# The seam between two parts of a TensorE-bound kernel: more of the second part's work woven into the first, and the seam's order written out

## The chip, the cores and the metric

The kernel runs on one NeuronCore of a Trainium2 chip. The core has TensorE (PE in the profile: matrix products, results into eight PSUM banks), VectorE (DVE), ScalarE (ACT), GpSimd (POOL) and SyncE (SP), whose queue issues nearly all DMAs here. Every engine works off its own queue in order and waits on semaphores for the others. The metric is device microseconds of the whole program, lower is better; most executions agree within 0.3%, those of this kernel within 0.05%.

## What is computed

The reference is one transformer layer over x of 16 sequences x 1024 positions x 512 channels, in float32, in two halves.

- Attention without softmax: q, k, v = x Wqkv^T + b; q and k are normalised by root mean square with gains gq, gk, rotated (rope), split into 16 heads of 32 and passed through relu. For each head, vk = sum over positions of [v, 1] k^T, and the output is vk q divided by its last row plus 1e-6. Then out = rmsnorm(attn Wout^T + b) gout, and x1 = layernorm(x + out).
- A feed-forward half with a shift in time: xk = mu_k x1 + (1 - mu_k) x1 of the position before (the same with mu_r for xr); r = sigmoid(xr W_r^T), k = relu(xk W_k^T)^2, and the result is layernorm(x1 + r * (k W_v^T)).

## The kernel before

The 16384 rows are N = 128 tiles of 128 positions; eight tiles make one sequence, of which there are NB = 16. Four tiles (512 positions) make one half-sequence s of the feed-forward, of which there are NH = 32. Every product of float32 numbers is made of three TensorE passes: each operand is split into a rounded high part (`..h`, written by ScalarE's copy) and the rest (`..l`, a VectorE or GpSimd subtraction), and high x high, high x low and low x high are added up. A 128 x 512 result over 512 channels is thus 12 matmuls of 512 columns.

**Part one** is `slot(i)` for i = 0 to 127, one slot per tile: `proj` makes q and k (24 matmuls, psq and psk), `rope` rotates them with tables that are loaded from DRAM for every slot (`tables`, one buffer for each of four), stores q to DRAM (`q_d`) and keeps k, scaled and through relu, as kh and kl. `add_kx(i - 1)` adds x^T k of the tile before to four PSUM banks (pskx, 12 matmuls). POOL keeps the sum of k over the sequence (`acc`). After a sequence's eighth tile, `finish_a` moves the four banks to SBUF (kx, high and low), `finish_s` makes the sums of k (psks, ksv), `finish_b` makes (Wv x^T) k (pskv: four groups g of four 256-wide and four 128-wide matmuls, two groups to a bank), adds the bias, and masks off what lies outside the heads, `finish_c` multiplies by Wout (psm) and stores the 512 x 512 matrix m of the sequence to DRAM (`m_d`), in four chunks. With m, the attention's output of a tile is q m. From slot 5 on, `late_weight` loads, splits and stores the feed-forward weights to DRAM, one chunk a slot.

Of **part two**, the attention's rest for a tile j is `part_q` (q through relu and divided by its denominator, VectorE), `part_qt` (four transposes, psqt, split into qth and qtl), `part_s` (a bank preset with the bias by ScalarE), `part_m` (12 matmuls, psy) and `part_y` (rmsnorm, residual, layernorm: a chain over DVE, ACT and POOL that ends with x1 in place of x). The feed-forward of half-sequence s is `part_t` (four times: `turn` makes four transposes of x1 into a bank, pst; `mix_t` makes xk or xr of one channel chunk in ScalarE and VectorE and splits it), `part_fk` (psk, relu, square), `part_fr` (psr, sigmoid) and `part_fv` (psv, gate, residual, layernorm, store). In the loop over s, attention runs two half-sequences ahead, one tile per step u, and `ffn` says which parts stand in which step.

Part two starts inside part one: at FIRST = 46 and every STEP = 8 slots, tile j = 0 to 6 (NPRE = 7) has its q and x loaded and `part_q`; for j below NDONE = 4 also `part_qt`, and one slot later `part_s`, `part_m`, `part_y`. Between the parts (the transition, lines 765 to 915) come the last add_kx and finish_*, the rest of tiles 4 to 9, and the first half-sequence's turns, mixes and psk.

Order: a scheduler places the instructions on each engine by a model of their times; `in_order(engine)` ties the instructions traced inside it to the order of the text. `issue_after(load.ins)` keeps DMAs behind a given one on SP. Memory comes from pools, taken and given back by the text; `ring` gives tile n of a tag one of `outer` buffers of an early pool or one of `inner` buffers of a pool opened later. `bank(name)` hands out the eight PSUM banks in turn: four from the pool `psum`, and once pskx is done four from `psumb`.

The lines that the change and the prediction touch: constants (22 to 26), `bank` (120), `load_m`, `load_ks`, `load_x` (190 to 206), `add_kx` (471 to 479), `finish_b` (532 to 543), the woven part of `slot` (739 to 755), `turn` and `mix_t` (778 to 803), `part_fk` (815), the transition (833 to 861), `ffn_first` (897) and the loop (903 to 934).

## Time and profile before

| | |
|---|---|
| median of three runs | 2735.54 us (2735.19 to 2736.36) |
| the profiled execution | 2735.11 us, span 2733.3 us |
| matmuls | 12558 |
| PE, PEld, DVE, ACT, POOL busy | 99%, 82%, 80%, 69%, 26% of the span |
| mean granted TensorE clock | 0.996 |
| moved by DMA | 431.18 MB, mean 158 GB/s |

The span runs from the first to the last instruction; the time of the execution is 1.8 us more. All times below are microseconds from the span's start. Part one takes the first 1195 us. A matmul's end in the profile is modelled: 512-wide ones last some 0.39 us each and start 0.227 apart, so a busy PE is not yet one at its peak, and a gap between two ends a little short of the time lost. PE's idle time before an instruction is put down to the engine that ended the wait. The row "granted clock" says what share of full speed TensorE's throttle allowed in a stretch. A line like L553 is a line of the kernel before; in the changed kernel the lines are shifted.

### The profile page before, as it was taken

The numbers are of one execution on the slowest core, as the hardware profiler recorded it, in microseconds if no ns is written. First come the engines' busy times: TensorE is split into PE (matmuls) and PEld (weight loads), VectorE is DVE, ScalarE is ACT, GpSimd is POOL, SyncE is SP. The second block draws the span as 40 slices with busy tenths as digits, with TensorE's granted clock in tenths as the row PEclk, the third lists the DMA queues.
The fourth block names the chain that finished last, engine by engine and source line by source line (L and its number), as shares of the span: only waits on it lengthen the run. The fifth ranks groups of instructions, "written<-read, shape, count | busy, mean of one in ns | idle before, by whom it ended". The sixth has DMA issues, their size and how long they took to land.

```text
span 2733.3 us, 40180 instructions
## 1 busy us (share of the span) xinstructions
PE 2693.3 (99%) x12558; PEld 2232.9 (82%) x12558; DVE 2190.7 (80%) x4879; ACT 1885.8 (69%) x3822; POOL 701.0 (26%) x801
## 2 busy tenths in 40 slices
PE   8999999999999999989999999999999999999998
PEld 6787888888888888867888888888888888888887
DVE  7887887888888877777887888888887888888874
ACT  6666665566666666567777777777777777777775
POOL 5222222222222222224322222222222222222221
PEclk9999999999999999999999999999999999999999
DMA  7698777777777777764222231323223232313210
GB/s 237 220 301 292 245 232 254 229 236 225 222 242 242 237 231 238 230 211 156 95 85 91 92 112 60 115 85 106 72 93 112 67 104 89 120 56 106 78 53 37
DMA packets 230862, 431.18 MB, mean 158 GB/s; under 512 B 24548, under 2 KB 24804, under 8 KB 230648
## 3 DMA queue, kind: packets, MB, share of 16 engines
q1 hardware_dynamic: 230352, 428.08, 48.7%
q8 instruction: 99, 1.62, 0.2%
q14 instruction: 115, 0.94, 0.1%
q10 hardware_dynamic: 296, 0.53, 0.1%
HBM read 313.15 MB, written 115.38 MB: 157 GB/s over the span
## 4 chain that ended last, share of the span: by engine, by line
PE 85%; DVE 6%; DMA 4%; issue 2%; ACT 2%; POOL 0%; SPq 0%; DVEq 0%; POOLq 0%; ACTq 0%
PE psk L178 13%; PE psv L178 13%; PE psr L178 13%; PE psy L178 12%; PE psq L407 9%; PE pskx L473 9%; PE psk L407 9%; PE pst L163 2%; PE psqt L163 2%; PE psm L553 1%; PE pskv L516 1%; DVE t L437 1%; DVE ro L439 1%; DMA m_d<-m 1%; DMA tab<-tab_d 1%
## 5 line engine op out<-in xcount | busy, mean ns | idle before, releaser
L178 PE MATMUL psk<-mkh,w_k 128*128 128x512 f32 x1024 | 333.3, 397 | 0.0
L178 PE MATMUL psv<-w_v,kah 128*128 128x512 f32 x1024 | 321.8, 395 | 0.0
L178 PE MATMUL psy<-mb,qth 128*128 128x512 f32 x1024 | 319.9, 389 | 0.2 <-ACT qth L233 0.2
L178 PE MATMUL psr<-w_r,mrh 128*128 128x512 f32 x1024 | 318.6, 396 | 0.0
L458 POOL TENSOR_TENSOR acc<-acc,ro 128x512 f32<-128x512 f32 x96 | 157.2, 1637 | 289.9 <-ACT ro L450 214.9
L178 PEld LDWEIGHTS psy<-mb,qth 128*128 128x128 f32 x1024 | 192.0, 188 | 40.2 <-ACT qth L233 0.4
L178 PEld LDWEIGHTS psk<-mkh,w_k 128*128 128x128 f32 x1024 | 192.2, 189 | 39.2
L142 POOL TENSOR_TENSOR rstd_all<-ss,mhalf 128x2 f32<-128x2 f32 x128 | 93.3, 729 | 501.2 <-DVE ss L444 481.0
L178 PEld LDWEIGHTS psr<-w_r,mrh 128*128 128x128 f32 x1024 | 188.8, 188 | 36.8
L178 PEld LDWEIGHTS psv<-w_v,kah 128*128 128x128 f32 x1024 | 187.8, 188 | 36.4
L800 POOL TENSOR_TENSOR mkl<-mixk,mkh 128x512 fp32r<-128x512 f32 x128 | 166.6, 1302 | 182.8 <-ACT mkh L799 182.8
L407 PE MATMUL psq<-wqk_h,xh 128*128 128x512 f32 x512 | 202.3, 395 | 6.4 <-ACT psq L157 4.6
L407 PE MATMUL psk<-wqk_h,xh 128*128 128x512 f32 x512 | 199.7, 390 | 1.8 <-ACT psk L157 1.7
L407 PE MATMUL psq<-wqk_l,xh 128*128 128x512 f32 x512 | 200.6, 392 | 0.7 <-DVE wqk_l L607 0.7
L178 PE MATMUL psk<-mkl,w_k 128*128 128x512 f32 x512 | 200.6, 392 | 0.0
L178 PE MATMUL psv<-w_v,kal 128*128 128x512 f32 x512 | 200.1, 391 | 0.0
L407 PE MATMUL psq<-wqk_h,xl 128*128 128x512 f32 x512 | 199.9, 390 | 0.0
L178 PE MATMUL psy<-mb,qtl 128*128 128x512 f32 x512 | 199.5, 390 | 0.1
L407 PE MATMUL psk<-wqk_h,xl 128*128 128x512 f32 x512 | 199.5, 390 | 0.0
L407 PE MATMUL psk<-wqk_l,xh 128*128 128x512 f32 x512 | 199.3, 389 | 0.0
L178 PE MATMUL psr<-w_r,mrl 128*128 128x512 f32 x512 | 196.7, 393 | 0.0
L142 POOL TENSOR_TENSOR yrs<-yss,mhalf 128x1 f32<-128x1 f32 x128 | 70.7, 552 | 383.5 <-DVE yss L273 275.3
(182 smaller groups left out, 7165.7 us busy)
## 6 DMA issues: line engine op xcount, KB each, us to landing
tab<-tab_d SPq DMA_DIRECT2D x480, 256.0 KB, 4.2
xt<-in_xt_dram SPq DMA_DIRECT2D x128, 256.0 KB, 4.0
xn<-in_x_dram SPq DMA_DIRECT2D x128, 256.0 KB, 3.7
q_d<-ro SPq DMA_DIRECT2D x128, 256.0 KB, 3.9
m_d<-m SPq DMA_DIRECT2D x64, 512.0 KB, 5.9
mb<-m_d SPq DMA_DIRECT2D x64, 512.0 KB, 7.0
q<-q_d SPq DMA_DIRECT2D x128, 256.0 KB, 2.9
x<-in_x_dram SPq DMA_DIRECT2D x128, 256.0 KB, 2.8
```

The costliest lines, as they stand in the source:

```text
L142: G.tensor_tensor(dst, src, mhalf[:, 0 : src.shape[1]], ALU.pow)
L163: T.matmul(ps[:, n * P : (n + 1) * P], lhsT=b, rhs=ident, is_transpose=True, start=(n == 0), stop=(n == NC_ - 1), skip_group_check=True,)
L178: T.matmul(ps, lhsT=a[u][:, rows], rhs=b[w][:, cols], start=(afresh and c == 0 and k == 0), stop=(c == n - 1 and k == 2), skip_group_check ...
L407: T.matmul(ps, lhsT=a[i][:, c, :], rhs=w_qk[b][:, c, cols], start=(not seeds and c == 0 and n == 0), stop=(seeds and c == NC_ - 1 and n == 2),
L437: V.tensor_mul(t2, ps[j], tab.pop((i, j, 1)))
L439: V.tensor_add(halves(r), halves(ps[j]), halves(t2)[:, :, ::-1, :])
L458: G.tensor_add(acc[b], acc[b], k)
L473: T.matmul(ps_kx[b][c], lhsT=a[:, c * P : (c + 1) * P], rhs=r, start=(t == 0 and n == 0), stop=(t == 7 and n == 2),)
L516: T.matmul(ps, lhsT=w_a["h"][:, c, cols], rhs=kx[:, c, g, :, :].rearrange("p two n -> p (two n)"), start=(g % 2 == 0 and c == 0), stop=Fal ...
L553: T.matmul(ps, lhsT=a[:, g, :], rhs=w_o[r][:, g, :], start=(n == 0), stop=(n == 2))
L800: (V if n == "r" and s != 1 else G).tensor_sub(ml, m, f32(mh))
```

## The change

More of part two goes into part one. FIRST is 30 instead of 46, and all eight tiles of the first sequence (NPRE = 8) are brought to x1 in part one. x1 of tiles 4 to 7 is stored to DRAM there (`x1_d`) and loaded again at the end of the transition. Three tiles of the second sequence (NQ = 3: tiles 8, 9, 10) have their q and x loaded and `part_q`, tile 8 also `part_qt`. A sequence's m is loaded one chunk a slot (slots 26 to 29 and 90 to 93) instead of four chunks at once. x has buffers in three places now: four and three in the early pool, four in the late one; weights are staged through the three (`xw`).

In the transition only tile 8's `part_m` and `part_y` are left of attention. Its order is fixed on TensorE (from the last slot on) and on ScalarE, VectorE and GpSimd: three turns and their mixes for k stand around the last `add_kx`; then `part_m(8)`, the finish steps, the fourth turn and mix, `part_y(8)`, psk00, the mixes for r, and psk01 to psk03 with `finish_c` between. `mix_t` is cut in two halves (`mix_a`, `mix_b`), `bank` takes a wished bank, and the pools of several tiles are exchanged so that w_k and w_r have other places; w_r is loaded after the finish steps. In `ffn_first` the products for r move forward by a step.

`add_kx` does a sequence's last tile bank by bank, three passes each, instead of pass by pass over the four banks. `finish_b` reads a PSUM bank only when both its groups are done.

The core of the diff:

```diff
-NPRE = 7
-FIRST, STEP = 46, 8
-NDONE = 4
-XA = 7
-XB = 4
+NPRE = 8
+NQ = 3
+FIRST, STEP = 30, 8
...
     def load_m(b, c):
-        ms[b, c] = ring("m", NC_ * b + c, NC_, 2, [P, 2, DIM], F32R, f"mb{b}{c}")
+        n = NC_ * b + c + (2 if b > 0 else 0)
+        ms[b, c] = ring("m", n, NC_, 2, [P, 2, DIM], F32R, f"mb{b}{c}")
...
-    def load_x(j):
-        xs[j] = ring("x", j, XA, XB, [P, DIM], F32, f"x{j}")
-        nc.sync.dma_start(out=xs[j], in_=x[j])
+    def load_x(j, src=None, early=False):
+        if early and j >= NT:
+            xs[j] = tp.tile([P, DIM], F32, tag="xw", bufs=3, name=f"xw{j}")
+        else:
+            xs[j] = x_tile(j)
+        nc.sync.dma_start(out=xs[j], in_=x[j] if src is None else src)
...
-            for n, (a, r) in enumerate(((h, kh), (l, kh), (h, kl))):
-                for c in range(NC_):
-                    T.matmul(
...
+            order = [(p, c) for p in three for c in range(NC_)]
+            if t == 7:
+
+                order = [(three[n], c) for c in range(NC_) for n in (0, 1, 2)]
+            for (n, a, r), c in order:
...
-                if g % 2 == 0:
-                    kv = te.tile([P, 2, P], F32, tag="kv", bufs=1, name=f"kv{b}{g}")
-                V.scalar_tensor_tensor(
-                    kv[:, g % 2, :], ks[:, cols], bv[:, g : g + 1], ps[:, 0:P], ALU.mult, ALU.add
-                )
                 if g % 2 == 1:
...
+                    for n in (g - 1, g):
+                        V.scalar_tensor_tensor(
+                            kv[:, n % 2, :],
...
+            if j + 1 in (0, NPRE) and late_by >= STEP - NC_:
+
+                with tc.issue_after(load.ins):
+                    load_m((j + 1) // 8, late_by - (STEP - NC_))
...
-                if late_by == 2 and j < NDONE:
+                if late_by == 2 and j < NPRE:
                     part_s(j)
                     part_y(j, part_m(j))
-
+                    if j >= NT:
+                        x1_d[j] = dram.tile([P, DIM], F32, name=f"x1_d{j}")
+                        nc.sync.dma_start(out=x1_d[j], in_=xs.pop(j))
...
+        end.enter_context(in_order(mybir.EngineType.PE))
+        slot(N - 1)
...
+            by_v = c == 3 if s == 0 and n == "k" else n == "r" and s != 1
+            (V if by_v else G).tensor_sub(ml, m, f32(mh))
...
         load_w("k", cb)
-        load_w("r", cb)
-        load_ks(1)
-        y5 = rest(NDONE)
+        chain = ctx.enter_context(ExitStack())
+        for e in ("Activation", "DVE", "Pool"):
+            chain.enter_context(in_order(getattr(mybir.EngineType, e)))
+        for c in range(3):
+            turn(0, c, c)
+        y8 = bank(f"psy{NPRE}", 3)
+        S.copy(y8, b_out)
+        seeds[NPRE] = y8
+        mix_a(0, 0, "k")
+        mix_a(0, 1, "k")
+        mix_b(0, 0, "k")
+        mix_a(0, 2, "k")
+        mix_b(0, 1, "k")
         add_kx(N - 1)
-        part_y(NDONE, y5)
+        part_m(NPRE)
         tk_ctx.close()
         finish_a(NB - 1)
+        mix_b(0, 2, "k")
         pa_ctx.close()
...
-        part_y(NDONE + 1, rest(NDONE + 1))
+        banks[0] = 4
         finish_s(NB - 1)
         finish_b(NB - 1)
-        first = 2 * NT
+        turn(0, 3)
+        mix_t(0, 3, "k")
         tx_ctx.close()
         wb = ctx.enter_context(tc.tile_pool(name="workb", reuse_waits="tile", bufs=1))
+        own["ks"] = wb
+        load_w("r", wb)
+        part_y(NPRE, y8)
+        part_fk(0, 0, 4)
         for c in range(NC_):
-            part_t(0, c)
-        part_y(NDONE + 2, rest(NDONE + 2))
-        for j in range(NPRE, first + 2):
-            load_q(j)
-        for g in range(NC_):
-            finish_c(NB - 1, g)
+            mix_t(0, c, "r")
+        chain.close()
+        part_fk(0, 1)
+        finish_c(NB - 1, 0)
+        finish_c(NB - 1, 1)
+        part_fk(0, 2)
+        finish_c(NB - 1, 2)
+        finish_c(NB - 1, 3)
+        part_fk(0, 3)
+        end.close()
...
+    for j in range(NT, NPRE):
+        load_x(j, src=x1_d[j])
+    load_w("v", wc)
```

More of the change, by code (lines that the diff above doesn't have):

```diff
@@ L118, with bank @@
     banks = [0]
-    def bank(name):
+    def bank(name, k=None):
+        if k is not None:
+            banks[0] = k
         k = banks[0] % 8
@@ L190, in load_m @@
     def load_m(b, c):
-        ms[b, c] = ring("m", NC_ * b + c, NC_, 2, [P, 2, DIM], F32R, f"mb{b}{c}")
+        n = NC_ * b + c + (2 if b > 0 else 0)
+        ms[b, c] = ring("m", n, NC_, 2, [P, 2, DIM], F32R, f"mb{b}{c}")
         nc.sync.dma_start(out=f32(ms[b, c]), in_=m_d[b][:, :, c, :])
     def load_ks(b):
-        ksb[b] = ring("ks", b, 1, 1, [P, DIM], F32, f"ksb{b}")
+        ksb[b] = ring("ks", b + (b > 0), 1, 1, [P, DIM], F32, f"ksb{b}")
         nc.sync.dma_start(
@@ L202, in load_q, with x_tile @@
         nc.sync.dma_start(out=qs[j], in_=q_d[j])
-    def load_x(j):
-        xs[j] = ring("x", j, XA, XB, [P, DIM], F32, f"x{j}")
-        nc.sync.dma_start(out=xs[j], in_=x[j])
+    def x_tile(j):
+        k = j % 11
+        if k < NT:
+            return tp.tile([P, DIM], F32, tag="x", bufs=NT, name=f"x{j}")
+        if k < 2 * NT:
+            return own["x"].tile([P, DIM], F32, tag="x", bufs=NT, name=f"x{j}")
+        return tp.tile([P, DIM], F32, tag="xw", bufs=3, name=f"x{j}")
+    def load_x(j, src=None, early=False):
[4 more added lines that the diff above has]
+        nc.sync.dma_start(out=xs[j], in_=x[j] if src is None else src)
     def heads(tl):
@@ L278, in part_y @@
         layernorm(xs[j], sm, f"a{j}")
-    def rest(j):
-        part_s(j)
-        part_qt(j)
-        return part_m(j)
     with ExitStack() as a_ctx:
@@ L329, with split_w @@
         w_o = {h: te.tile([P, NC_, DIM], F32R, name=f"wout_{h}") for h in "hl"}
-        def split_w(hi, lo, src, low, dma, tag="x", bufs=XA):
+        def split_w(hi, lo, src, low, dma, tag="xw", bufs=3):
             w = tp.tile([P, DIM], F32, tag=tag, bufs=bufs, name="wstage")
@@ L470, in add_kx @@
                 ]
-            for n, (a, r) in enumerate(((h, kh), (l, kh), (h, kl))):
-                for c in range(NC_):
-                    T.matmul(
-                        ps_kx[b][c],
-                        lhsT=a[:, c * P : (c + 1) * P],
-                        rhs=r,
-                        start=(t == 0 and n == 0),
-                        stop=(t == 7 and n == 2),
-                    )
+            three = ((0, h, kh), (1, l, kh), (2, h, kl))
+            order = [(p, c) for p in three for c in range(NC_)]
+            if t == 7:
+                order = [(three[n], c) for c in range(NC_) for n in (0, 1, 2)]
+            for (n, a, r), c in order:
+                T.matmul(
+                    ps_kx[b][c],
+                    lhsT=a[:, c * P : (c + 1) * P],
+                    rhs=r,
+                    start=(t == 0 and n == 0),
+                    stop=(t == 7 and n == 2),
+                )
         fin, ksv = {}, {}
@@ L531, in finish_b @@
                     )
-                if g % 2 == 0:
-                    kv = te.tile([P, 2, P], F32, tag="kv", bufs=1, name=f"kv{b}{g}")
-                V.scalar_tensor_tensor(
-                    kv[:, g % 2, :], ks[:, cols], bv[:, g : g + 1], ps[:, 0:P], ALU.mult, ALU.add
-                )
                 if g % 2 == 1:
                     two = slice(g - 1, g + 1)
-                    low = both.rearrange("p (g two n) -> p g two n", g=2, two=2)[:, :, 1, :]
-                    V.tensor_add(kv, kv, low)
+                    kv = te.tile([P, 2, P], F32, tag="kv", bufs=1, name=f"kv{b}{g}")
+                    low = both.rearrange("p (g two n) -> p g two n", g=2, two=2)
+                    for n in (g - 1, g):
+                        V.scalar_tensor_tensor(
+                            kv[:, n % 2, :],
+                            ks[:, n * P : (n + 1) * P],
+                            bv[:, n : n + 1],
+                            low[:, n % 2, 0, :],
+                            ALU.mult,
+                            ALU.add,
+                        )
+                    V.tensor_add(kv, kv, low[:, :, 1, :])
                     V.tensor_mul(kv, kv, mask.unsqueeze(1).to_broadcast([P, 2, P]))
@@ L597, in stage_qk @@
             n = NC_ * j + c
-            w = tp.tile([P, DIM], F32, name="wstage", **[dict(tag="x", bufs=XA), dict(tag="q", bufs=3)][n >= XA])
+            w = tp.tile([P, DIM], F32, name="wstage", **[dict(tag="x", bufs=NT), dict(tag="xw", bufs=3), dict(tag="q", bufs=3)][(n >= NT) + (n >= NT + 3)])
             dma.dma_start(out=w, in_=wqkv[:, c, j * DIM : (j + 1) * DIM])
@@ L739, in slot @@
             j, late_by = divmod(i - FIRST, STEP)
-            if 0 <= j < NPRE:
+            if j + 1 in (0, NPRE) and late_by >= STEP - NC_:
+                with tc.issue_after(load.ins):
+                    load_m((j + 1) // 8, late_by - (STEP - NC_))
+                    if late_by == STEP - 1:
+                        load_ks((j + 1) // 8)
+            if 0 <= j < NPRE + NQ:
+                b = j // 8
                 if late_by == 0:
                     with tc.issue_after(load.ins):
-                        if j == 0:
-                            load_ks(0)
-                            for c in range(NC_):
-                                load_m(0, c)
                         load_q(j)
-                        load_x(j)
+                        load_x(j, early=j < NPRE)
                 if late_by == 1:
                     part_q(j)
-                    if j < NDONE:
+                    if j <= NPRE:
                         part_qt(j)
-                if late_by == 2 and j < NDONE:
+                if late_by == 2 and j < NPRE:
                     part_s(j)
                     part_y(j, part_m(j))
+                    if j >= NT:
+                        x1_d[j] = dram.tile([P, DIM], F32, name=f"x1_d{j}")
+                        nc.sync.dma_start(out=x1_d[j], in_=xs.pop(j))
+        x1_d = {}
         tp.tile([P, 56], F32, name="fill_top")
-        for i in range(N):
+        for i in range(N - 1):
             slot(i)
@@ L761 @@
                 start_pe.close()
+        end = ctx.enter_context(ExitStack())
+        end.enter_context(in_order(mybir.EngineType.PE))
+        slot(N - 1)
         i_ctx.close()
@@ L766 @@
         wm = ctx.enter_context(tc.tile_pool(name="workm", reuse_waits="tile", bufs=1))
-        own["ks"] = wm
         w_f = {}
@@ L776, with turn, mix_a @@
         mix, turned = {}, {}
-        def turn(s, c):
-            ps = bank(f"pst{s}{c}")
+        def turn(s, c, k=None):
+            ps = bank(f"pst{s}{c}", k)
             transposes(ps, [xs[NT * s + t][:, c * P : (c + 1) * P] for t in range(NT)])
             turned[s, c] = ps
-        def mix_t(s, c, n):
+        mixed = {}
+        def mix_a(s, c, n):
             ps = turned[s, c]
             m = wm.tile([P, HT], F32, tag="mix", bufs=3, name=f"mix{n}{s}{c}")
+            mixed[s, n, c] = m
             S.activation(m, ps, AF.Copy, scale=mu[n][:, c : c + 1])
@@ L795, in mix_t, with mix_b @@
                 )
-            pool, bufs = (wm, 5) if n == "k" else (wb, 6)
-            mh = pool.tile([P, HT], F32R, tag=f"m{n}h", bufs=bufs, name=f"m{n}h{s}{c}")
-            ml = pool.tile([P, HT], F32R, tag=f"m{n}l", bufs=bufs, name=f"m{n}l{s}{c}")
+        def mix_b(s, c, n):
+            ps = turned[s, c]
+            m = mixed.pop((s, n, c))
+            bufs = 5 if n == "k" else 6
+            mh = wm.tile([P, HT], F32R, tag=f"m{n}h", bufs=bufs, name=f"m{n}h{s}{c}")
+            ml = wm.tile([P, HT], F32R, tag=f"m{n}l", bufs=bufs, name=f"m{n}l{s}{c}")
             S.copy(mh, m)
-            (V if n == "r" and s != 1 else G).tensor_sub(ml, m, f32(mh))
+            by_v = c == 3 if s == 0 and n == "k" else n == "r" and s != 1
+            (V if by_v else G).tensor_sub(ml, m, f32(mh))
             mix[s, n, c] = mh, ml
@@ L803, in mix_t @@
                 V.tensor_copy(halo[:, c : c + 1], ps[:, HT - 1 : HT])
+        def mix_t(s, c, n):
+            mix_a(s, c, n)
+            mix_b(s, c, n)
         def part_t(s, c):
@@ L813, in w_pair, with part_fk @@
             return w_f[n][:, c, 0, :], w_f[n][:, c, 1, :]
-        def part_fk(s, o):
-            ps = bank(f"psk{s}{o}")
+        def part_fk(s, o, k=None):
+            ps = bank(f"psk{s}{o}", k)
             product(
@@ L823, in part_fk @@
             )
-            r = wm.tile([P, HT], F32, tag="r", bufs=2, name=f"r{s}{o}")
+            r = wb.tile([P, HT], F32, tag="r", bufs=2, name=f"r{s}{o}")
             S.activation(r, ps, AF.Relu)
@@ L897 @@
     ffn_first = (
-        (("r", 0),),
-        (("t", 0), ("r", 1), ("t", 1), ("r", 2)),
-        (("r", 3), ("t", 2), ("v", 0), ("t", 3), ("v", 1)),
+        (("r", 0), ("r", 1)),
+        (("r", 2), ("t", 0), ("r", 3), ("t", 1)),
+        (("t", 2), ("v", 0), ("t", 3), ("v", 1)),
         (("v", 2), ("v", 3)),
     )
-    for j in range(NPRE, first + 1):
-        load_x(j)
-    for c in range(NC_):
-        load_m(1, c)
-    for j in range(NPRE, first):
-        part_q(j)
-        part_y(j, rest(j))
-    for o in range(NC_):
-        part_fk(0, o)
-    load_w("v", wc)
-    part_q(first)
-    part_qt(first)
     for s in range(NH):
@@ L918 @@
             j = NT * (s + 2) + u
-            if j + 2 < N:
+            if NPRE + NQ <= j + 2 < N:
                 load_q(j + 2)
-            if j + 1 < N:
+            if NPRE + NQ <= j + 1 < N:
                 load_x(j + 1)
                 part_q(j + 1)
-            if j < N:
+            if NPRE < j < N:
                 part_s(j)
@@ L932 @@
             if j < N:
-                ps = part_m(j)
+                if j > NPRE:
+                    ps = part_m(j)
                 if j + 1 < N:
                     part_qt(j + 1)
-                part_y(j, ps)
+                if j > NPRE:
+                    part_y(j, ps)
                 if j % 8 in (6, 7) and j // 8 + 1 < NB:
```

## The prediction

> **What bounds the kernel now.** First the page's busy table:

> ```profile
> PE 2693.3 (99%) x12558; PEld 2232.9 (82%) x12558; DVE 2190.7 (80%) x4879; ACT 1885.8 (69%) x3822; POOL 701.0 (26%) x801
> ```

> TensorE is busy throughout, and only 40.0 us of the span (2733.3) are without a matmul. The same 12558 matmuls stand in the changed program, so the change can win only in those 40 us, and in time at a lower clock. Second, the busy times by stretch show where the loss is; the columns are length, then busy us and instructions of PE, PEld, DVE, ACT and POOL, then granted clock, DMA share, GB/s:

> ```profile
> 441.00:746.00 305.00, 302.61 (x1397) 251.13 (x1397) 248.31 (x449) 186.60 (x395) 69.08 (x68) 1.00 0.74 233
> 1000.00:1189.00 189.00, 189.00 (x882) 158.25 (x881) 149.96 (x260) 112.70 (x237) 45.39 (x40) 1.00 0.73 231
> 1189.00:1300.00 111.00, 96.52 (x457) 78.67 (x456) 81.06 (x194) 76.96 (x150) 40.51 (x41) 0.95 0.49 171
> 1300.00:2700.00 1400.00, 1400.00 (x6631) 1161.89 (x6630) 1142.73 (x2986) 1065.41 (x2122) 356.17 (x475) 1.00 0.27 88
> ```

> Line two is part one with nothing woven in: no idle. Line one is the stretch where four tiles are woven: 2.4 us idle. Line three is the transition: 14.5 us idle, and a clock of 0.95. Line four is part two: none. Third, who ends TensorE's waits in the transition, and the clock around the longest of them:

> ```profile
> PE psm L553 <- ACT kvth L542: 7.3, 1, 7.3
> PE psqt L163 <- DVE q L222: 4.3, 2, 3.2
> PE pskv L516 <- DVE kv L534: 1.5, 1, 1.5
> ...
> 1220.50:1223.90 3.40, 0.93 (x8) 0.79 (x7) 3.40 (x10) 1.27 (x3) 0.55 (x1) 1.00 0.41 130
> 1223.90:1234.10 10.20, 5.34 (x13) 4.18 (x14) 9.03 (x20) 5.92 (x11) 3.71 (x3) 0.50 0.22 85
> ```

> In the 7.3-us wait VectorE has no idle time: `finish_b`'s short products stand in its queue among the first sequence's mixing and layernorms. The wait also halves the clock for 10.2 us.

> The sum lost in the transition: the timeline gives the usual start-to-start spacing as 0.227 us for a 512-wide matmul, 0.171 for 256, 0.06 for 128, 0.109 for a transpose. From 1189 to 1300 start 350, 16, 16 and 72 of them: 91.0 us for a stretch of 110.6. **19.6 us are lost**: 14.5 idle, about 2.4 by the half clock (13 matmuls in 5.34 us), the rest small stalls and refilling after each gap.

> **The change, part by part.** The built program's order and its waits give the new sequence; I time it with rows of before, from the end of psk127 (1194.84).

> *Transition, TensorE's order*: kx126, three transposes of the first sequence, kx127 bank by bank, psy8, psks, 32 pskv, pst03, psk00, psk01, two psm, psk02, psm, then psr and the rest. Its waits:

> (a) kx127. kh is ready at 1198.52 as before; before it kx126 (12 x 0.227) and 12 transposes (12 x 0.109) fill to 1198.65. Bank by bank, the third matmul already needs kl: kh's end + ACT's ro (0.73) + DVE's kl (0.68) = 1199.95, two matmuls after 1198.65. Wait 0.85 (today 0.21, since eight matmuls with kh come first).

> (b) psks. psy8 ends at 1204.96. ACT first does three mixes, two casts, four kx copies (0.48 apart) and mkh02, so the copy of ma ends at 1205.6 and DVE's half follows. That DVE subtraction falls on POOL's mkl02 (1205.1 to 1206.4). Row: the mrl subtraction that began at 1224.96 beside POOL's mkl (1224.60 to 1225.86) took 1.45 us where the next took 0.68. Wait 1.2 without a collision, 1.9 with; I take 1.9. [...]

> (c) psk00. pskv takes 16 x (0.171 + 0.06) = 3.7, to 1211.0; DVE and ACT then do two kv chains in strict order (2 x 0.34, 0.41, 0.41, ACT 0.40, DVE 0.41, some 0.05 between each), and only then the fourth mix (ACT 0.69, DVE 0.74, ACT 0.62, DVE 0.68). mkh03 is there at 1216.1, mkl03 at 1216.8; TensorE has pst03 and nine matmuls of psk00, to 1213.55. Waits 2.6 and 0.5: 3.1.

> (d) The second psm writes psk00's bank, so it waits for ACT's Relu of psk00. In ACT's queue that stands behind tile 8's whole layernorm. Row: tile 4's chain at 1203.90, without its queueing, takes 5.2 us from y to the last activation, plus 0.7 to the next ACT start and 0.6 for the Relu: 1216.7 + 6.6 = 1223.3. psk01 and one psm fill to 1220.7. Wait 2.6.

> (e) The third psm takes psk02's bank, so it waits for the Relu of psk02, in ACT's queue eight instructions after the first Relu and behind POOL's kal00 (1.29): 5.0 after it, against psm + psk02 (3.4) on TensorE. Wait 1.65.

> Sum (a) to (e): 10.1 us. Each misses some semaphore time; bounds 9 to 14.

> *Clock.* Rows: a 3.4-us stretch with 2.62 us idle (25.8 to 29.2) was followed by one at 0.50, so was 1220.5 to 1223.9 (2.47 idle); 104.3 to 107.7 with 1.60 idle was not. Waits (c) and (d) can each do it, by where they fall; after (c) the slack of (d) hides it, after (d) it costs at most half of 3.4. I take 0.5, bounds 0 to 3.4. [...]

> *Loads in the transition.* w_r now waits on SP behind ks_d15's store, and is issued near 1207.5 instead of 1197.1; psr00 needs it near 1228: hidden. The four tiles stored in part one come back after the last psm's store, near 1235, w_v behind them. Row: w_v's second chunk landed at 1258.07, 12.4 us after the first was issued, with 2.5 MB before and around it, 0.28 MB/us. 3.9 MB from 1234.6 land by 1248.5; psv wants the first chunk at 1248.7, the last at 1250.7. Between 0 and 4 us; I take 0.4, and 0.3 for the q tiles that cost 4.3 us today: of them only tile 11's q is still on VectorE here, q8 to q10 are made in part one.

> Transition: 10.1 + 0.5 + 0.7 = **11.3 lost instead of 19.6: 8.3 us won**, bounds 4 to 11.

> *Part one.* Four more tiles (eight, from slot 30) bring no TensorE work that is not taken out later. But they cost more here: eight slots with a tile take 76.3 us (starts of psq46, 54, 62, 70, 78), without one 72.25 (86 to 126), and a tile's matmuls are 12 x 0.227 + 4 x 0.109 = 3.2. So 0.9 is lost per tile, 3.6 today. Of this 1.6 are three waits of pskv between its halves:

> ```profile
> PE pskv L516 <- DVE ro L439: 1.6, 3, 0.8
> PE pskx L473 <- DVE kl L451: 0.6, 1, 0.6
> ```

> There TensorE waits until VectorE has read the first half of a bank. Now both reads come after both halves, and all 32 pskv stand in one run: I let these waits go (also one of 0.28 at 201.9). What is late next is kv, but its psm comes a slot later. Left are 0.5 a tile, eight times: 4.0. With the 0.28 the net is nothing; I take 0.8 lost, bounds -2 (no loss by tiles) to +4 (0.9 for each of eight).

> *At nothing*: m in single chunks, the wider x ring and w staged through three buffers: DMA share is 0.74 here, and m is wanted slots later. The four stores (0.3 us of SP each) stand before the next slot's two k tables; the table was issued at 635.86, tile x2's normalisation beside it ended at 634.69, so the store is through first. If that cover goes: landing takes 4.2, the table was used at 641.75, so 1.7 us more of slack. From psr21 on TensorE's order is the same to the end.

> The profiled execution took 2735.11 (span 2733.3), 0.4 under the median 2735.54. 2735.5 - 8.3 + 0.8 = **2728.0**.

> **The rivals.** *No change that counts*: the chains (b) to (e) are longer by their semaphores, (d) and (e) each bring a half-clock stretch, w_v is late. 19.6 - 16 = 3.6 won, 0.8 lost in part one: 2732.7. For it: five serial waits on four queues held to one order; against it: each duration is a row. *Slower*: a store of a spilled tile holds SP. If tile 4 to 7's normalisation ends over 2.9 us (1.2 + 1.7) later against the table's issue than x2's did, TensorE waits for rope. To pass 2741 the four would have to cost (8.3 + 5.5) / 4 = 3.4 us each, so end 6.3 us later; with that price 2741.5, at double 2755. For it: DVE is 81% busy there and SP issues in order; against it: the row is of just this slot pattern. *The wait only moves*: w_v and the returning tiles 4 us late: 2731.6; against it: the landing worked out above.

> **How the numbers follow.** About 0.2% (5.5 us) is what this kernel's measurement tells from no change. The forecast, 2723 to 2730, has 0.66, and is all of faster. No change has 0.15 and the moved wait 0.07; both end within the bound. Slower has 0.12: the spill 0.10, other bad orders of part one 0.02. The likeliest's own bounds are 2735.5 - 11 - 2 = 2722.5 and 2735.5 - 4 + 4; for 8 in 10 I take 2721 to 2738, which leaves out the spill's upper half and little below.

> **What would show it.** Right: from psk127 to psr00 no wait above 3.4 us; waits before kx127's third matmul, psks, psk00's tenth, the second and third psm, ended by DVE kl, DVE ma, ACT mkh, ACT r, ACT r; no pskv wait in part one; clock at 1.00 but for at most one or two stretches. Wrong: a wait for a DMA on TensorE (w_v, x), waits in slots 64 to 90 ended by tables or ro, or a part one that grows by more than the 12.7 us of the four tiles' own matmuls plus 4.

## The result, and the profile after

The changed kernel takes 2727.55 us (median of 13 runs, 2725.43 to 2732.18), the kernel before in the same comparison 2733.17 (13 runs, 2730.28 to 2736.76). The ratio is 0.9979, with a 95% interval of 0.9971 to 0.9988: 5.6 us won by the medians, a little more than the 0.2% that can be told from no change. The forecast was 2728.0, worked out as 7.5 us won from 2735.54, the median of three runs. Thirteen runs of the kernel before lie 0.24% apart, not 0.05% as those three did, and their median is 2.4 us lower: that the forecast time comes within 0.5 us is in part luck, the win itself was 1.9 us smaller than forecast. The profiled execution took 2727.38 us (span 2725.6), 7.7 us less than the profiled one of before, which was among the slower of its kernel.

The busy table of the changed kernel's page:

```profile
PE 2692.8 (99%) x12558; PEld 2233.1 (82%) x12558; DVE 2169.7 (80%) x4880; ACT 1881.5 (69%) x3822; POOL 699.8 (26%) x800
```

These are the same matmuls, with 32.8 us of the span without one instead of 40.0. The busy times by stretch, with the columns as before (length, PE, PEld, DVE, ACT, POOL, granted clock, DMA share, GB/s):

```profile
280.00:310.00 30.00, 26.90 (x117) 21.28 (x116) 21.96 (x41) 16.29 (x35) 6.89 (x6) 1.00 0.86 283
310.00:615.00 305.00, 305.00 (x1417) 254.85 (x1416) 245.48 (x459) 190.75 (x402) 71.85 (x69) 1.00 0.74 232
615.00:880.00 265.00, 265.00 (x1240) 221.74 (x1239) 211.65 (x399) 166.06 (x352) 62.34 (x61) 1.00 0.75 237
880.00:920.00 40.00, 38.70 (x171) 31.69 (x170) 30.12 (x55) 22.24 (x48) 8.29 (x9) 1.00 0.80 258
1203.00:1314.00 111.00, 104.44 (x494) 84.94 (x493) 75.56 (x174) 77.41 (x151) 40.72 (x39) 0.98 0.43 145
1227.00:1230.40 3.40, 1.11 (x5) 0.50 (x3) 2.05 (x5) 1.61 (x3) 0.00 (x0) 1.00 1.00 393
1230.50:1233.90 3.40, 3.17 (x8) 2.48 (x8) 1.91 (x6) 0.69 (x2) 0.56 (x1) 0.51 0.07 25
1314.00:2700.00 1386.00, 1386.00 (x6561) 1150.12 (x6560) 1129.49 (x2955) 1057.64 (x2104) 348.83 (x467) 1.00 0.28 89
```

Lines two and three are the slots with a woven tile: no idle at all, where before had 2.4 us in four tiles. Lines one and four are new: here a sequence's m is loaded, and TensorE stands idle for 3.1 and 1.3 us. Line five is the transition, 6.6 us idle instead of 14.5; lines six and seven are its longest wait and the half clock after it. The waits of TensorE in the transition, with who ended them (us in total, times, longest):

```profile
PE psk L178 <- ACT mkh L831: 2.3, 1, 2.3
PE psm L570 <- ACT r L863: 2.1, 2, 1.3
PE psks L511 <- DVE ma L508: 0.9, 1, 0.9
PE pskx L485 <- DVE kl L459: 0.7, 1, 0.7
PE psk L178 <- DVE mkl L833: 0.2, 1, 0.2
PE pskx L485 <- ACT kh L457: 0.2, 1, 0.2
```

These are waits (a) to (e) of the prediction, each at its place and ended by the engine that was named for it; the two psm waits, (d) and (e), are one line, and the last line, for kh, stood in the kernel before too.

Time lost is counted below as in the prediction: starts of matmuls further apart than 0.227, 0.171, 0.06 and 0.109 us. Up to the end of psk127 the kernel before lost 26.9 us, the changed one 27.7; in the transition 19.65 and 10.8. So 8.8 us were won in the transition, 0.8 lost in part one (between two profiled executions; the medians differ by less); from there to 2700 TensorE is never idle in either. The experiments show that this agreement with the forecast holds for the sum of part one only, not for its terms.

### The profile page after: what moved, and what is told of

Same layout as the page of the kernel before. It is cut to its first block, busy times and chain, and to the rows that moved or that the text cites. A ratio compares the mean times of both kernels' runs of the same rounds, so it can differ in the third digit from the quotient of the medians.

```text
span 2725.6 us, 40197 instructions
## 1 busy us (share of the span) xinstructions
PE 2692.8 (99%) x12558; PEld 2233.1 (82%) x12558; DVE 2169.7 (80%) x4880; ACT 1881.5 (69%) x3822; POOL 699.8 (26%) x800
## 4 chain that ended last, share of the span: by engine, by line
PE 86%; DVE 1%; DMA 1%; ACT 1%; issue 0%; POOL 0%; SPq 0%; POOLq 0%; DVEq 0%; ACTq 0%
PE psr L178 13%; PE psv L178 13%; PE psy L178 13%; PE psk L178 13%; PE psq L415 9%; PE pskx L485 9%; PE psk L415 9%; PE psqt L163 2%; PE pst L163 2%; PE psm L570 1%; PE pskv L528 1%; DMA tab<-tab_d 0%; PE pskv L536 0%; DMA ksb<-ks_d 0%; DMA q<-q_d 0%
```

## The experiments

Each is timed beside the kernel before. The last four columns give the us lost in a stretch, from the profiled execution of each; the transition is from psk127 to 110 us later. The kernel before takes 2733.2 to 2735.0 in these comparisons. Between 60 and 280 us, where the instructions of all kernels made from the changed one (the second excepted) are alike, they lost 8.9 to 11.3 us: single executions differ by some 2 us there, so a kernel's total is told by its median, and the cause by its stretch.

| kernel | median us | ratio to before, 95% | 280-310 | 310-880 | 880-920 | transition |
|---|---|---|---|---|---|---|
| before | 2733.17 | 1 | 0.0 | 4.2 | 0.0 | 19.65 |
| e6 before, new finish_b | 2725.69 | 0.9967 (0.9954-0.9979) | 0.0 | 0.1 | 0.0 | 16.0 |
| changed | 2727.55 | 0.9979 (0.9971-0.9988) | 3.9 | 0.1 | 1.6 | 10.8 |
| e2 old finish_b | 2730.88 | 0.9991 (0.9982-1.0000) | 1.1 | 3.7 | 0.0 | 14.2 |
| e1 m at once | 2726.72 | 0.9971 (0.9962-0.9980) | 0.2 | 3.0 | 1.6 | 10.8 |
| e9 ks later | 2725.05 | 0.9969 (0.9957-0.9980) | 1.3 | 0.6 | 0.4 | 10.8 |
| e12 m behind x | 2727.90 | 0.9978 (0.9970-0.9987) | 2.5 | 2.1 | 1.1 | 10.8 |
| e7 stores twice | 2728.53 | 0.9979 (0.9968-0.9989) | 6.3 | 1.2 | 1.2 | 10.8 |
| e3 pass by pass | 2728.26 | 0.9983 (0.9974-0.9992) | 2.3 | 0.7 | 0.9 | 10.8 |
| e5 ma first | 2727.68 | 0.9976 (0.9968-0.9985) | 5.7 | 0.6 | 0.6 | 10.1 |
| e10 mix between | 2728.98 | 0.9982 (0.9973-0.9991) | 4.5 | 0.4 | 0.5 | 13.8 |
| e13 Relu early | 2727.79 | 0.9982 (0.9973-0.9991) | 5.9 | 0.5 | 0.3 | 10.0 |
| e14 all | 2719.22 | 0.9951 (0.9938-0.9963) | 4.1 | 0.1 | 0.1 | 5.1 |
| e16 all, m at once | 2717.94 | 0.9937 (0.9923-0.9951) | 0.5 | 0.9 | 0.0 | 5.1 |

**The kernel before with the new finish_b alone.**

```diff
-                if g % 2 == 0:
-                    kv = te.tile([P, 2, P], F32, tag="kv", bufs=1, name=f"kv{b}{g}")
-                V.scalar_tensor_tensor(
-                    kv[:, g % 2, :], ks[:, cols], bv[:, g : g + 1], ps[:, 0:P], ALU.mult, ALU.add
-                )
                 if g % 2 == 1:
+                    kv = te.tile([P, 2, P], F32, tag="kv", bufs=1, name=f"kv{b}{g}")
+                    for n in (g - 1, g):
+                        V.scalar_tensor_tensor(kv[:, n % 2, :], ...)
```

> The kernel before, with the new finish_b alone (a bank of pskv is read only when both its groups are done). Theory (the three pskv waits in part one come from the read between the halves): the waits at 484.5 (0.76), 561.9 (0.63) and 714.3 (0.25) go, the stretch 430 to 760, which loses 4.3 us, loses some 2.5; in the transition the pskv wait of 1.5 goes, but kvth, for which psm waits 7.3, comes no sooner, so the sum there stays within 0.7. Total 1.5 to 2.5 less than the kernel before: ratio 0.9992. Rival (it is the edit that carries the gain): 5 us or more less, the transition's loss under 15. Third: the waits move to the psm behind: no gain.

Measured: 2725.69 us (5 runs; before 2733.68), ratio 0.9967 (0.9954 to 0.9979). The rival is right: this edit alone wins as much as the whole change (the two intervals overlap). Its profile, at the woven part and the transition:

```profile
430.00:600.00 170.00, 170.00 (x785) 141.65 (x785) 135.95 (x254) 104.97 (x221) 39.35 (x38) 1.00 0.76 246
600.00:760.00 160.00, 160.00 (x742) 133.66 (x741) 127.17 (x237) 100.70 (x211) 38.80 (x37) 1.00 0.72 235
1182.00:1293.00 111.00, 101.49 (x475) 81.80 (x474) 81.15 (x197) 78.13 (x155) 42.80 (x43) 0.97 0.50 173
```

From 430 to 760, 0.2 us are lost instead of 4.3: beside the three pskv waits (1.64) a wait of pskx behind them (0.61) goes, and the refilling after each. In the transition 16.0 are lost instead of 19.65 (the rival's under 15 was not reached). The reason is seen in when ScalarE makes the two halves of kvth, first in the kernel before, then in this one (the line gives the starts of the first and the last):

```profile
L542 ACT CAST kvth<-kv x2: 399/404/408, 1216.7 to 1228.3; 128x256 fp32r<-128x256 f32 x2
```

```profile
L547 ACT CAST kvth<-kv x2: 404/426/448, 1207.0 to 1212.1; 128x256 fp32r<-128x256 f32 x2
```

11.6 us between the two halves became 5.0. With the read between the halves, each half of pskv had its own place in VectorE's queue to wait for, and the scheduler put other work between: in the kernel before, the second half of pskv150 starts at 1212.5, 2.2 us after pskv152 began to fill, and its VectorE steps stand at 1213.6, 1214.5 and 1216.2. The 7.3-us wait of psm came from that order, not from the amount of work, which is the same in both. Shorter waits took its place: the first products for k (psk) wait five times, 4.9 us in all, mostly for the mixes, psqt waits 2.6, and the clock still halves twice (0.51 from 1226.3 to 1229.7, 0.65 from 1242.4 to 1245.8).

**The changed kernel with the old finish_b**, the same lines the other way.

> The changed kernel with the old finish_b (a bank of pskv is read after each of its groups). The kernel before with the new finish_b alone lost 4.1 us less in its woven part and 3.6 less in the transition. Theory (finish_b is most of what the change wins): here the pskv waits come back in the slots with a woven tile, 310 to 880 loses 4 to 8 us instead of 0.1, the transition 0 to 2 more: 2731 to 2737, no faster than the kernel before. Rival (it counts only beside the old transition, by the order that the scheduler makes of it): under 2 us more, 2727 to 2729.5.

Measured: 2730.88 us, 3.3 more than the changed kernel; 310 to 880 loses 3.7 instead of 0.1, the transition 14.2 instead of 10.8. The waits in part one:

```profile
PE pskv L528 <- DVE ro L447: 0.9, 3, 0.5
PE pskv L528 <- DVE kv L546: 0.5, 1, 0.5
```

By its stretches the edit is worth 7 us here too; by the medians 3.3, just under the 2731 to 2737 that was expected. Its order of instructions also loses less before 310 (6.7 from 60 to 280, 1.1 from 280 to 310), and its profiled execution (2727.03) is the fastest of its eleven. The first theory holds in the main: without this edit the rest of the change is not shown to win anything (0.9991, the interval reaches 1).

**m and ks: at once; ks a slot later; behind the x tile.**

```diff
-            if j + 1 in (0, NPRE) and late_by >= STEP - NC_:
-                with tc.issue_after(load.ins):
-                    load_m((j + 1) // 8, late_by - (STEP - NC_))
-                    if late_by == STEP - 1:
-                        load_ks((j + 1) // 8)
...
                     with tc.issue_after(load.ins):
+                        if j in (0, NPRE):
+                            load_ks(b)
+                            for c in range(NC_):
+                                load_m(b, c)
                         load_q(j)
```

That is the edit of the first. The second moves `load_ks` alone to that place; the third leaves the lines where they are and has them issued after the load of xn.

> The changed kernel, but with the four chunks of a sequence's m and its ks loaded at once with the woven tile's q (slots 30 and 94), as the kernel before did it at slot 46, instead of a chunk a slot in slots 26 to 29 and 90 to 93. Theory (the chunks ride in the slots in which m of another sequence is stored, and push the x tile for add_kx late): the waits before pskx at 293.5 (1.23 us), 297.3 (1.86) and 902.5 (1.30) go; the stretches 280 to 310 and 880 to 920, which lose 3.9 and 1.6 us, lose under 1 each; one new wait of some 0.6 behind the four chunks, as before's kernel had it at 489.2. Sum 3 to 5 us less than the changed kernel: about 2723.5. Rival (the stores of m and the q and x of the woven tile are enough to fill the queue): the waits stay or move by a slot, 2727 to 2728.

> The changed kernel, with m still loaded a chunk a slot, but ks (whose issue holds SP for 1.23 us in slot 29) loaded one slot later, with the woven tile's q. If the long issue of ks on SP is what makes the x tile late: the waits at 293.5 and 297.3 (3.1 us together) go, the one at 902.5 too; 2723 to 2724.5. If it is the bytes (0.94 of the DMA engines busy, 277 GB/s, between 280 and 300): they stay within 0.5 us, 2727 to 2728.

> The changed kernel, with the chunks of m and ks issued behind the slot's x tile for add_kx instead of behind its xt tile, so that in each of the slots 26 to 29 and 90 to 93 the x tile is not held by them on SP or in the queues. Theory (of the 4.4 us waited at 293.5, 297.3 and 902.5, the long issue of ks was one part, the rest is the chunk ahead of the x tile): these waits go, 280 to 310 and 880 to 920 together lose under 1.5 us (5.5 in the changed kernel, 1.7 with ks a slot later): 2723 to 2724.5. Rival (the bytes of these slots fill the queue whatever the order): the waits stay above 1 us or come back at the tables for rope, which now stand behind the chunk: 2726 to 2729.

In the changed kernel the x tile for add_kx (xn, one buffer) is what comes late. ScalarE's split of it, between 284 and 304:

```profile
L331 ACT CAST xnh<-xn x2: 614/616/617, 293.5 to 301.8; 128x512 fp32r<-128x512 f32 x2
...
  DMA xn<-in_x_dram: 4.6, 1
```

ScalarE stands idle 4.6 us before it, with kh28 behind it in its queue, and pskx waits for kh28 and kl28. The tile's load stands on SP behind the chunk, two tables, a store of another sequence's m and ks (SP is 1.2 us on ks), and is issued at 284.90. With m at once, in a kernel that runs 2.2 us ahead at this place, it is issued at 281.55 and split at 287.7, so 1.2 and 3.6 us sooner, and the stretch loses 0.2. The two issues, changed kernel first (start, us on SP):

```profile
284.90 1.13 SPq L324 DMA_DIRECT2D xn<-in_x_dram  x1
```

```profile
281.55 0.35 SPq L324 DMA_DIRECT2D xn<-in_x_dram  x1
```

That a full queue alone does not do it shows in the next lines, 290 to 300 in the changed kernel and then with m at once:

```profile
290.00:300.00 10.00, 6.90 (x29) 4.88 (x29) 6.53 (x12) 4.52 (x10) 2.00 (x2) 1.00 0.89 321
```

```profile
290.00:300.00 10.00, 10.00 (x46) 8.28 (x45) 6.43 (x11) 5.19 (x11) 3.76 (x3) 1.00 0.99 354
```

More moves, and TensorE does not wait. All traces together tell the chunk from ks. From the issue of the x tile's load one slot before to the split of this tile, the nine kernels with the chunk ahead of the load take 16.5 to 20.0 us, e9 (17.1) and e14 (17.8) among them, which have ks a slot later; the three without it ahead (e1, e12, e16) take 13.9 to 14.4. The issue of ks itself takes SP 0.32 us in e9's slot (and 0.32 in the median of the 16 in the changed kernel), so its 1.2 is not a price of ks. But loading both at once cost 3.0 us elsewhere (single waits of pskx of 0.35 to 0.94, such as single kernels have now and then) and left 880 to 920 at 1.6, so e1 missed its 2723.5. With ks a slot later the first stretch lost 1.3 in one kernel (2725.05 us, between the two ranges expected) and 4.1 in another (e14), against 2.3 to 6.3 in the six with the changed kernel's loads: the two ranges overlap, and ks alone isn't shown to be the cause. Putting the loads behind xn brought this tile in time but moved the wait a slot on, to 302.5 (1.7 us), and the kernel stayed at 2727.90: its theory fell.

**Each spilled tile's store twice.** A second identical store behind the first.

> The changed kernel, with each of the four stores of a spilled tile's x1 issued twice. Theory (a store costs SP 0.3 us, and there are some 3 us between it and the need of the next table): the stretch 620 to 880, in which the four stores stand, loses 0.1 to 0.5 us more; time as the changed kernel, 2727 to 2728. Rival (the stores hold SP or the queue): a new wait of 0.3 us or more in each of the four slots, 1.5 to 6 us more, ended by tables or by ro.

It took 2728.53 us. There is no wait for tables or ro in 620 to 880, which loses 0.1 (one wait of 0.76 stands at 602.6, before the first of these stores). The stores are hidden, so the prediction's slower rival had no ground here.

This trace also shows what the half clock behind wait (c) costs. Its waits in the transition are those of the changed kernel, but (c) is divided between two stretches of the 3.413-us grid on which the clock changes in the traces of before and of the changed kernel (measured in the last section), the second of them with 1.83 us of matmuls, and the clock stays at 1.00:

```profile
1231.24:1234.65 3.41, 1.83 (x7) 1.30 (x8) 1.97 (x4) 1.31 (x3) 0.00 (x0) 1.00 0.52 204
```

Wait (d) is 2.30 here instead of 0.83, and the transition loses 10.8 in both: in this order the half clock is hidden.

**add_kx pass by pass**: the two lines of `order` for t == 7 taken out.

> The changed kernel, with a sequence's last add_kx pass by pass over the four banks again, as the kernel before has it. Theory (wait (a) is kl's, and it is paid once only because the next wait stands behind another chain): the wait of 0.75 before kx127's third matmul goes, TensorE comes 0.9 earlier to psks, and the wait for ma there grows from 1.0 to 1.9, since ScalarE starts the copies of the four banks at 1216.6 behind the mixes and VectorE's ma ends at 1221.0 in either case. Time within 0.5 us of the changed kernel. Rival (a) counts by itself: 0.9 us less. Third: the last bank is ready later and holds the copies: 0.5 to 1 us more.

The wait (a) for kl is gone, and psks waits as much longer:

```profile
PE psks L508 <- ACT ma L504: 1.1, 1, 1.1
PE psks L508 <- DVE ma L505: 0.9, 1, 0.9
```

The transition loses 10.8 as before. (a) was real as a wait, and worth nothing: what follows is set by ScalarE's and VectorE's chain.

**ScalarE's mkh02 behind finish_s.**

```diff
         finish_a(NB - 1)
-        mix_b(0, 2, "k")
...
         finish_s(NB - 1)
+        mix_b(0, 2, "k")
         finish_b(NB - 1)
```

> The changed kernel, with ScalarE's copy mkh02 placed behind finish_s, so that POOL's mkl02 cannot run beside VectorE's subtraction for ma and the copy of ma comes 0.6 us earlier on ScalarE. Theory (b): VectorE's ma, 1.35 us beside mkl02, takes 0.68; psks waits 0.3 to 0.5 instead of 1.0; what follows comes 0.7 us earlier: 2726.8. Rival (the subtraction is long for another reason): it takes 1.3 again, the wait stays near 1.0, no gain. Third: mkl02 now meets VectorE's kv steps and makes them longer, 0.3 to 0.7 us lost again at wait (c).

VectorE's subtraction for ma, in the changed kernel beside POOL's mkl02, then here without it:

```profile
L508 DVE TENSOR_TENSOR ma<-acc,ma x1: 1350/1350/1350, 1219.7 to 1219.7; 128x512 fp32r<-128x512 f32 x1
```

```profile
L508 DVE TENSOR_TENSOR ma<-acc,ma x1: 679/679/679, 1221.4 to 1221.4; 128x512 fp32r<-128x512 f32 x1
```

The wait fell from 1.0 to 0.5, the transition by 0.75, as worked out; it can't be seen in the median. In the changed kernel mkl02 runs from 1219.22 to 1220.50, and the subtraction that began at 1219.69 ends 0.55 after it. Here mkl02 ran beside VectorE's kv steps (1223.8 to 1225.1), which read PSUM: they took 344 ns, as without it (345).

**The fourth mix between the two kv chains.**

```diff
-        def finish_b(b):
+        def finish_b(b, between=None):
...
+                if g == 3 and between is not None:
+                    between()
                 if g % 2 == 1:
...
-        finish_b(NB - 1)
-        turn(0, 3)
-        mix_t(0, 3, "k")
+        finish_b(NB - 1, lambda: (turn(0, 3), mix_t(0, 3, "k")))
```

> The changed kernel, with the fourth turn and its mix put between the two kv chains of the last finish_b instead of behind both; TensorE's order is the same as far as psm. Theory (c) is the fourth mix, held behind two kv chains: mkh03 comes at about 1227.6 instead of 1230.0, so the waits in psk00 (2.29 + 0.23) shrink to 0.7. But the second kv chain and tile 8's layernorm end no sooner, so ScalarE's Relus of psk00 and psk02 stay where they are or come 1.2 us sooner at most: most of the gain of 1.8 reappears at the second and third psm, and the transition loses 9.2 to 10.4 instead of 10.4. Rival (the waits are independent): the transition loses 8.5 or less. Third: the half clock now falls on a later wait and is not hidden: 11 or more.

Wait (c) fell from 2.5 to 0.4. But:

```profile
PE psm L572 <- ACT r L865: 4.1, 1, 4.1
PE psm L572 <- DVE nma L271: 1.7, 1, 1.7
```

```profile
1237.80:1241.20 3.40, 0.00 (x0) 0.00 (x0) 0.72 (x1) 3.17 (x7) 1.25 (x2) 1.00 0.33 130
1241.90:1245.30 3.40, 3.40 (x9) 2.62 (x10) 2.09 (x5) 3.37 (x7) 1.65 (x2) 0.50 0.01 2
```

All of the gain went into one wait for the Relu of psk02, which ended when it did before; that wait covers a whole stretch of 3.4 us, and TensorE ran at a clock of 0.50 for 6.8 us after it, with no wait behind to hide it. By the spacing of the starts this costs 3.0 us, the whole difference between 13.8 lost and 10.8: the third case.

**The Relus ahead of tile 8's layernorm.**

```diff
-        part_y(NPRE, y8)
         part_fk(0, 0, 4)
-        for c in range(NC_):
-            mix_t(0, c, "r")
-        chain.close()
+        mix_t(0, 0, "r")
         part_fk(0, 1)
         finish_c(NB - 1, 0)
         finish_c(NB - 1, 1)
+        part_y(NPRE, y8)
+        chain.close()
+        mix_t(0, 1, "r")
         part_fk(0, 2)
         finish_c(NB - 1, 2)
         finish_c(NB - 1, 3)
+        mix_t(0, 2, "r")
+        mix_t(0, 3, "r")
         part_fk(0, 3)
```

> The changed kernel, with the end of the transition in another order on ScalarE, VectorE and GpSimd: psk00 with its Relu and the first r mix ahead of tile 8's layernorm, which comes behind psk01 and the first two finish_c; the other r mixes stand around psk02 and no longer hold a strict order. Theory (d) and (e) are Relus held in ScalarE's queue behind other work, not ScalarE being full: the waits before the second and third psm (0.83 and 1.27) go, with their refilling; a wait of at most 0.5 comes at psk02. Transition 7.5 to 8.5 lost instead of 10.4: 2725.5. Rival (ScalarE and VectorE are full, as moving only the fourth mix suggested): the r mixes come later by as much and psr00 waits; 9.5 to 11 lost, no gain.

Waits (d) and (e) are gone, and 1200 to 1255 loses 8.0 instead of 10.4. But 65 us further on a product for r (psr) now waits for a Relu (1.16), in an order that the scheduler made; together 10.0 are lost, and the median doesn't show it.

**All of these, then with the first m at once.** Last: the order just shown, with the fourth mix between, mkh02 behind finish_s and ks a slot later; and the same with the first sequence's m in slot 30.

> The order of the last one, and with it the mix between the kv chains, mkh02 behind finish_s, and ks a slot later. Theory (the fourth mix early pays once the Relus no longer stand behind the layernorm): psks waits 0.5, psk00 0.4 to 0.7, no psm waits over 0.5, psk02 1.4 at most for its bank; no wait is long enough to halve the clock. Transition 4.5 to 6 lost instead of 10.4; 280 to 310 and 880 to 920 together 1 to 2.5 instead of 5.5: 2718.5 to 2721.5. Rival (the sum of ScalarE's work sets the end of the transition): as with the mix alone, one wait of 3 to 4 us behind psk02 and the half clock behind it, 9 to 12 lost: 2724 to 2727.

> The last kernel (all the changes of the transition's end), with the first sequence's m loaded at once in slot 30, the second's still a chunk a slot. Theory (the chunks beside the stores of another sequence's m are what holds the x tile in slots 26 to 30): 280 to 310 loses under 1 us, where it lost 1.3 to 6.3 in the seven kernels with the chunks a slot; the rest as in the last kernel: 2715 to 2718. Rival (the loss follows the load to the next slots, as some waits of 0.3 to 0.9 did with both at once): 310 to 880 loses 1 to 3 more, 2718 to 2720.

e14: 2719.22 us. Its waits in the transition (three more are of 0.2), and the stretch itself:

```profile
PE psk L178 <- ACT mrh L833: 1.0, 1, 1.0
PE pskx L485 <- DVE kl L459: 0.7, 1, 0.7
PE psks L511 <- DVE ma L508: 0.5, 1, 0.5
```

```profile
1200.00:1311.00 111.00, 108.08 (x523) 88.70 (x522) 79.44 (x179) 79.53 (x155) 43.49 (x42) 1.00 0.44 149
```

No wait over 1.0, and the clock is 1.00 throughout. Alone, the three edits changed the transition by -0.75, +3.0 and -0.8; together by -5.7. The theory of (c), (d) and (e) as one chain holds for the mix: alone its gain came back before psm, with the half clock on top; here no psm waits. The Relus early won 2.4 alone too, and 1.6 of it was lost again at the wait of psr; why the order of e14 has no such wait is not shown. From 280 to 310 it lost 4.1, more than expected.

e16: 2717.94 us, ratio 0.9937. That stretch now:

```profile
280.00:310.00 30.00, 29.75 (x132) 24.33 (x131) 22.05 (x43) 16.83 (x36) 8.05 (x7) 1.00 0.98 343
```

It loses 0.5; 310 to 880 loses 0.9, so the rival has a part. By medians e16 is not told from e14 (their intervals overlap); the stretch tells them apart. This kernel is faster than both: than the kernel before by 17.1 us in its own comparison (2735.03), than the changed one by 9.6 by the two medians.

## Why the prediction was right, and where its steps were not

- **(a)** 0.85 forecast, 0.75 measured, ended by kl as said. As a term of the sum it was wrong to count: e3 shows that without it (b) is longer by about the same.
- **(b)** 1.9 forecast with the collision, 1.0 measured (0.11 + 0.89). The collision was there, 1350 ns against 679. TensorE came to psks 0.6 later than worked out (psy8's last matmul began at 1219.2, so the next could have at 1219.4, not at 1204.96 + 13.86 = 1218.8 on this kernel's clock), so less of the chain was left to wait for. e5 shows both sides for this pair of engines: VectorE's subtraction of two SBUF tiles took 1350 ns beside POOL's mkl02 and 679 without it, the kv steps, which also read PSUM, 344 beside it and 345 without. In the trace of before VectorE's kl, at 1200.23 beside POOL's acc, took 0.68: kl had started ahead of acc there, and acc paid, 1.84, where it takes 1.30 when it starts first.
- **(c)** 3.1 forecast, 2.5 measured (2.29 and 0.23); mkh03 came at 1230.0 as worked out (1216.1 + 13.86), mkl03 too.
- **(d)** The second psm began at 1237.2 as forecast. The wait was 0.83, not 2.6: the half clock after (c) made psk01 3.76 us long instead of 2.73, and the rest of TensorE's way there had its own refilling. The prediction had said that the slack of (d) hides the half clock after (c); e7, where (d) waits 2.30 at full clock, shows that it did.
- **(e)** 1.65 forecast, 1.27 measured; psm at 1242.2 as forecast.
- **Clock.** The transition has one half-clock stretch, 0.51 from 1230.5 to 1233.9, after 2.29 us of idle in 3.4, as the rows of before had it (2.62 and 2.47 idle). The 3.4 us ahead of it were only partly idle: five matmuls stand in them.
- **Loads.** w_r, w_v and the returning tiles held nobody; the 0.7 forecast for them wasn't there. The rate for w_v was misread: 2.5 MB in 12.4 us are 0.20 MB/us, not 0.28, and the trace of before moves 314 GB/s in that stretch.
- **The sum.** 11.3 lost forecast, 10.8 measured, with parts that fit less well. From start to start, the five waits cost 0.9, 1.4, 3.0, 1.0 and 1.4, together 7.7 instead of 10.1; the half clock costs 1.6 instead of 0.5, and (d) is shorter by as much; loads cost nothing instead of 0.7; and 1.5 are the wait for kh and the refilling after each wait, which were named but not priced. That the sum came so near is partly luck.
- **Part one** came out at the forecast 0.8 lost, by two errors that cancel. The working itself gave a net of nothing, and 0.8 was chosen inside wide bounds, so to meet it is luck. "Left are 0.5 a tile, eight times: 4.0" failed: between 310 and 880 the woven tiles lost 0.1. The 0.9 a tile of before was nearly all the read between the halves, and I had priced it at its three waits (1.64) alone; e6 measures 4.1. "At nothing: m in single chunks" failed the other way: 3.9 and 1.6 us between 280 and 310 and between 880 and 920. I had taken DMA share 0.74 as cover, but the slots of the chunks are those in which another sequence's m is stored, and the load of xn, which has one buffer, stands behind the chunk in the same queue.
- **What won.** I gave finish_b 1.6 + 0.28 and the written order of the transition nearly all. e6 shows finish_b at 10.6 us in the profiles (7.0 in part one, of which 4.1 in the woven part and most of the rest before 280, where executions differ anyway; 3.6 in the transition) and 8.0 in the medians, as much as the whole change; inside the changed kernel (e2) it is worth 3.3 by the medians. From there, the weave and the new order win 5.2 in the transition and lose 7.8 in part one, 5.5 of it at the chunks. I had looked at the 7.3-us wait and seen VectorE full; the edit alone took it away, with the short steps now set sooner in VectorE's queue. So the forecast of "faster" was right, but its main source of gain was mis-sized.
- **Rivals.** No change: the chains were not longer by their semaphores. Slower by spilled stores: e7 finds no cost. The wait moving to w_v or x: not there; but e3 and e10 show waits that move from link to link of the same chain.

Open: why, with the chunk ahead of xn in both and ks a slot later, one kernel lost 1.3 us and another 4.1; and why single waits of pskx of up to 1.3 us come in other slots of some kernels. A second buffer for xn wasn't tried.

## What to carry to other kernels

A consumer that reads a PSUM bank between two halves of its filling cost twice here: in waits (three of 1.6 us together between 441 and 746 in the kernel before), and by a place in another engine's queue around which the scheduler must order everything else (11.6 us between the halves of kvth, 5.0 without it); try that edit alone first. In a chain over three in-order queues, price a fix by the last link, not by the wait it removes: alone, two of three fixes were worth 0.8 us each and the third cost 3.0, together they were worth 5.7. A mean DMA share of 0.74 (441 to 746 in the kernel before) did not make the loads of m free here (3.9 and 1.6 us lost in their slots): look at the slot, at what else is issued in it, and at which tile with a single buffer stands behind.
